# Layer 2 of a four-layer cross-attention kernel: another mask instruction, the layer norm on other engines, the weights transposed one tile later, and its last tiles beside layer 3

## The chip, the cores and the metric

The kernel runs on one core of one Trainium2 chip. Its engines work side by side, each through its own instructions in order: TensorE (PE in the profile, with its weight loads as PEld), VectorE (DVE), ScalarE (ACT), GpSimd (POOL) and SyncE (SP), which issues the DMAs here. They wait for each other by semaphores. The metric is the time of one execution in device microseconds; less is better.

## The reference

Four layers of cross-attention follow each other on x (4 batches, 1024 rows of 256); the context has 77 rows in each batch. The change is in layer 2 and at its seam with layer 3:

```python
# layer 2: 16 heads of 16; mask and factors come as inputs (4, 16, 1024, 77)
scores = einsum('bhqd,bhkd->bhqk', q, k) / sqrt(16) * attention_weights
scores = where(attention_mask, -inf, scores)
out = softmax(scores) @ v                       # heads side by side again
x = x + out @ Wo.T + bo
x = (x - mean(x)) * rsqrt(var(x) + 1e-5) * gamma + beta
# layer 3: 16 heads of 64, no mask
normed = x * rsqrt(mean(x * x) + 1e-6) * norm_w
x = x + softmax((normed @ wq) @ (ctx @ wk).T) @ (ctx @ wv) @ wo
```

Layers 0 and 1 (self- and cross-attention with a feed-forward part; Taylor linear attention with a window) take the first three quarters of the time and are not touched.

## The kernel before, in words

The order of all work is written out by hand; the instructions of each engine stand in the order of the program text. Layers 2 and 3 work in tiles of 128 rows, 32 in all, eight to a batch. The output projection is folded into the values beforehand (`U`: one row of 256 for each head and context row), so a tile has one score matrix `s` of 128 x 1232 (16 heads of 77), its transpose `pT` in ten pieces, and one product `po` of `pT` with `U`.

A function `slots` calls `slot2` for i = 0 to 34 and then `slot3` for i = 0 to 33. One call is called a slot; it issues parts of several tiles. `slot2(i)` issues, in this order:

- the loads of factors and mask (`side`) for tile i+1, and a new `s` for tile i (one of three buffers; POOL clears its last 48 columns, L1288);
- for tile i-1 sixteen exponentials on ScalarE, one for each head, with the maximum `nm` as bias (L1363);
- for tile i the scores on TensorE (`ps`, L45), the product with the factors on VectorE (L1375, two halves, from PSUM), and the mask in one VectorE instruction: mask times -1e30 plus s (L1380; the mask is of 8-bit numbers);
- side jobs up to a given share of the batch (`gap2`);
- for tile i-3 the product `po` (ten matrix multiplies, shown as twenty records);
- for tile i the maximum of each head (L1392, L1396);
- for tile i-2 the ten transposes `psT` (L1283) and their three copies out of PSUM on ScalarE (L1284);
- for tile i-3 the addition of `po` to x on VectorE (L1402) and of the bias row `bo` on GpSimd (L1403);
- side jobs again;
- for tile i-1 the sums and their reciprocals on VectorE (L1408, L1409), and the scaling of `s` by them on GpSimd (L1410).

Side jobs are generators, each advanced in small steps between two given shares of a batch of eight slots. In layer 2 they are: `prep2` (transposes x of the next batch, `ptx`, copied by VectorE, L340, and projects it, `pp`, copied by ScalarE, L1332); `norm2(b-1)`, the layer norm of the batch before, which begins at share 0.45 with `bn_stats` and `bn_aggr` of eight tiles on VectorE (L298, L299), goes on with a short chain on GpSimd that makes rs = (var + 1e-5) to the power -0.5 (L289, L290), and then treats one tile a step by two VectorE instructions (L1421, L1425); and during the last batch the first batch of layer 3, `stats3(0)` and `features3(0)` (L313, `ptx`, L342). `norm2` of the last batch is a job of layer 3's first batch.

`slot3(i)` is alike, with a lag of two: scores `ps` with `G`, maximum and subtraction on VectorE (L1480, L1481), one exponential for all heads (L1489), sums, reciprocals and scaling (L1492 to L1494), transposes, `po`, the addition (L1504) and the store of the finished tile.

PSUM has two tiles for `ps` (`pair_tile`), three for `psT`, `ptx` and `pp` together, and one for `po`; so a `po` begins only when L1402 has read the one before.

Of the kernel before, what the change touches and what calls it, by code (L numbers as in the profile page):

```python
# [10 lines left out]
F32 = mybir.dt.float32  # L11
# [20 lines left out]
def tile_xattn_seq(ctx: ExitStack, tc: tile.TileContext, d: dict, out: bass.AP):  # L32
# [65 lines left out]
    def load_cols_of(*keys):  # L98
        for key, n in keys:
            cols[key] = cpool.tile([P, n], F32, name="c_" + key)  # L100
            load_cols(cols[key], d[key])

    load_cols_of(("L0_xattn_g1", 2), ("L0_xattn_be1", 2))
    nhalf = cpool.tile([P, NT], F32, name="nhalf")
    nc.gpsimd.memset(nhalf, -0.5)

# [1177 lines left out]
        nc.scalar.copy(pT[:, 4 * group : 4 * group + n, :], ps[:, 0:n, :])  # L1284

    def new_scores():
        s = late.tile([P, P * NC], F32, name="s", tag="s", bufs=3)
        nc.gpsimd.memset(s[:, HK:], 0.0)  # L1288
        return s

# [56 lines left out]

    def slot2(i, tiles, at, gap2):

        p1, p2, p3 = tiles.get(i - 1), tiles.get(i - 2), tiles.get(i - 3)  # L1350
        a = None
        if i < NB * NT:
            b, t = divmod(i, NT)
            a = tiles[i] = dict(b=b, t=t)
            qT, kb = shared["b2", b], shared["k2"]
            fs, mk = shared.pop(("side", i))
            if i + 1 < NB * NT:
                load_sides(i + 1)
            s = a["s"] = new_scores()
        if p1:  # L1360
            for h in range(H):
                hs = p1["s"][:, S * h : S * h + S]
                nc.scalar.activation(hs, hs, AF.Exp, bias=p1["nm"][:, h : h + 1], scale=SC)  # L1363
        if a:
            for o in range(2):
                ps = pair_tile()
                for e in range(2):
                    r = half_rows(e)
                    mm(
                        ps[:, e, 0 : 4 * S].rearrange("p (h s) -> p h s", s=S),  # L1370
                        qT[r, o, P * t : P * t + P],
                        kb[r, o, :, b, :],
                    )
                so = slice(o * HH * S, (o + 1) * HH * S)
                nc.vector.tensor_tensor(  # L1375
                    s[:, so].rearrange("p (i n) -> p i n", i=2), ps[:, :, 0 : 4 * S],
                    fs[:, so].rearrange("p (i n) -> p i n", i=2), ALU.mult,
                )
            sv = s[:, 0:HK]
            nc.vector.scalar_tensor_tensor(sv, mk, NEG, sv, op0=ALU.mult, op1=ALU.add)  # L1380
        gap2(at + 0.4)
        if p3:
            U = shared["u2", p3["b"]]
            xt = xs[p3["b"]][:, p3["t"], :]
            po = pvp.tile([P, D], F32, name="po2", tag="pv")
            for c in range(NC):
                r = slice(0, rows_in(c))
                mm(po, p3["pT"][r, c, :], U[r, c, :], start=(c == 0), stop=(c == NC - 1))
            del tiles[i - 3]
        if a:  # L1390
            nm = a["nm"] = small.tile([P, H], F32, name="nm", tag="m16")
            nc.vector.tensor_reduce(  # L1392
                nm, sv.rearrange("p (h k) -> p h k", k=S), axis=AX.X, op=ALU.max
            )

            nc.vector.tensor_scalar(nm, nm, 0.1 * NEG, -SC, ALU.max, ALU.mult)  # L1396
        if p2:
            pT = p2["pT"] = late.tile([P, NC, P], F32, name="pT", tag="pT")
            for g in range(3):
                turned(p2["s"], g, pT)  # L1400
        if p3:
            nc.vector.tensor_tensor(xt, po, xt, ALU.add)  # L1402
            nc.gpsimd.tensor_tensor(xt, xt, rows["bo"], ALU.add)  # L1403
        gap2(at + 1.0)
        if p1:
            s3 = p1["s"][:, 0:HK].rearrange("p (h k) -> p h k", k=S)
            den = small.tile([P, H], F32, name="den", tag="den")
            nc.vector.tensor_reduce(den, s3, axis=AX.X, op=ALU.add)  # L1408
            nc.vector.reciprocal(den, den)  # L1409
            nc.gpsimd.tensor_tensor(  # L1410
                s3, s3, den.unsqueeze(2).to_broadcast([P, H, S]), ALU.mult
            )

    def norm2(b):

        x = xs[b]
        res = []
        yield from stats_job(res, lambda t: x[:, t, :], 1e-5, False)
        mv, rs = res
        for t in range(NT):  # L1420
            nc.vector.scalar_tensor_tensor(  # L1421
                x[:, t, :], x[:, t, :], mv[:, t, 0:1], rows["gamma"],
                op0=ALU.subtract, op1=ALU.mult,
            )
            nc.vector.scalar_tensor_tensor(  # L1425
                x[:, t, :], x[:, t, :], rs[:, t : t + 1], rows["beta"],
                op0=ALU.mult, op1=ALU.add,
            )
            yield


# [23 lines left out]
    def slot3(i, tiles, at, gap2):  # L1455
        a, p2 = None, tiles.get(i - 2)
        if i < NB * NT:
            b, t = divmod(i, NT)
            a = tiles[i] = dict(b=b, t=t)
            G, _ = shared["b3", b]  # L1460
            xT = shared["xT3", b]
            s = a["s"] = new_scores()
            m = small.tile([P, H], F32, name="m3", tag="m16")
        if p2:
            pT = late.tile([P, NC, P], F32, name="pT", tag="pT")
        for o in range(2):
            if p2:
                turned(p2["s"], o, pT)
            if a:
                ps = pair_tile()  # L1470
                for e in range(2):
                    k0 = (2 * o + e) * 4 * S
                    for c in range(2):
                        mm(
                            ps[:, e, 0 : 4 * S], xT[:, c, P * t : P * t + P],
                            G[:, c, k0 : k0 + 4 * S], start=(c == 0), stop=(c == 1),
                        )
                pv = ps[:, :, 0 : 4 * S].rearrange("p i (h s) -> p i h s", s=S)
                mo = m[:, HH * o : HH * o + HH].rearrange("p (i h) -> p i h", i=2)
                nc.vector.tensor_reduce(mo, pv, axis=AX.X, op=ALU.max)  # L1480
                nc.vector.tensor_tensor(  # L1481
                    s[:, HH * S * o : HH * S * (o + 1)].rearrange("p (i h s) -> p i h s", i=2, s=S),
                    pv, mo.unsqueeze(3).to_broadcast([P, 2, 4, S]), ALU.subtract,
                )
        if p2:
            turned(p2["s"], 2, pT)
        gap2(at + 0.5)
        if a:
            nc.scalar.activation(s[:, 0:HK], s[:, 0:HK], AF.Exp)  # L1489
            s3 = s[:, 0:HK].rearrange("p (h k) -> p h k", k=S)  # L1490
            den = small.tile([P, H], F32, name="den", tag="den")
            nc.vector.tensor_reduce(den, s3, axis=AX.X, op=ALU.add)  # L1492
            nc.vector.reciprocal(den, den)  # L1493
            nc.gpsimd.tensor_tensor(  # L1494
                s3, s3, den.unsqueeze(2).to_broadcast([P, H, S]), ALU.mult
            )
        if p2:
            U = shared["b3", p2["b"]][1]
            xt = xs[p2["b"]][:, p2["t"], :]
            po = pvp.tile([P, D], F32, name="po3", tag="pv")  # L1500
            for c in range(NC):
                r = slice(0, rows_in(c))
                mm(po, pT[r, c, :], U[r, c, :], start=(c == 0), stop=(c == NC - 1))
            nc.vector.tensor_tensor(xt, po, xt, ALU.add)  # L1504
            nc.sync.dma_start(out=out[p2["b"], P * p2["t"] : P * p2["t"] + P, :], in_=xt)
            del tiles[i - 2]
        gap2(at + 1.0)
# [156 lines left out]
    run(loads2(0))  # L1664
    run(prep2(0))

    def slots(slot, lag, jobs_of):
        tiles = {}
        for i0 in range(0, NB * NT + lag, NT):
            b = i0 // NT  # L1670
            jobs = jobs_of(b)
            n = min(NT, NB * NT + lag - i0)

            def gap2(share):
                for j in jobs:
                    j.run(share / n)

            for k in range(n):
                slot(i0 + k, tiles, k, gap2)
            for j in jobs:  # L1680
                j.end()

    def jobs2(b):
        j = []
# [11 lines left out]
    def jobs3(b):  # L1696
        j = []
        if b == 0:
            j.append(Job(norm2(NB - 1), 16, 0.0, 1.0))
        if b + 1 < NB:  # L1700
            j.append(Job(stats3(b + 1), 8, 0.0, 0.4))
            j.append(Job(features3(b + 1), 8, 0.45, 0.95))
            j.append(Job(loads3(b + 1), 1, 0.4, 0.41))
        return j

    slots(slot2, 3, jobs2)
    slots(slot3, 2, jobs3)


# [28 lines left out]
```

## Time and profile before

| | |
|---|---|
| median of three runs | 2509.88 us (2508.1 to 2509.99) |
| the profiled execution | time 2512.11 us, span 2510.4 us |
| PE, DVE, ACT, POOL busy over the span | 92%, 58%, 41%, 24% |
| first mask of layer 2 | 1880.1 us |
| last `po` of layer 2 ends | 2190.5 us |
| DMA over the span | 39 GB/s on the mean |

All profile times are of the one profiled execution; microseconds count from the start of its span. In the windows each row gives a stretch, its length, the busy time of each engine with the number of instructions, the granted TensorE clock (1 is full), the share of DMA, and GB/s. In the groups a row is one line of the kernel on one engine: output and inputs by name, shapes and count, then busy time, the mean ns of one, and the idle time of that engine before them with what ended it. The waits name who waited for whom. The timeline gives start and duration of single instructions or of a few of one kind, merged.

### The profile page before, as it was taken

Reading aid. Unit: us, or ns where it says so; the run is one execution under the profiler, and the core shown is the slowest. Engines: PE = TensorE matmul, PEld = TensorE weight load, DVE = VectorE, ACT = ScalarE, POOL = GpSimd, SP = SyncE. Lnnn points to the kernel's source line nnn. Section 1 sums busy time; section 2 is a strip of 40 time slices with the busy share of each in tenths; the row PEclk is TensorE's granted clock in tenths of the full one; section 3 lists DMA queues with packets and bytes.
Section 4 is the critical chain, followed back from the end, with each engine's and each line's share of the span. In section 5 each row is a group of like instructions: output and inputs, shape, how many; then the busy total and the mean of one; then the engine's idle time right before and its main releaser. Section 6 shows DMA issues by size and latency. Waiting matters only on the chain.

```text
span 2510.4 us, 39752 instructions
## 1 busy us (share of the span) xinstructions
PE 2301.8 (92%) x16162; PEld 1387.1 (55%) x16162; DVE 1446.8 (58%) x2411; ACT 1019.0 (41%) x1684; POOL 595.5 (24%) x850
## 2 busy tenths in 40 slices
PE   5789989898989989899999999999988997899999
PEld 3433433444444444444556766656656665678887
DVE  4446456654565444664346435454438999797664
ACT  1234344333443344334443434444436665322222
POOL 2001013111130111311152223333323333332222
PEclk9799999999999999999999999999998999899999
DMA  6412021100000000100000010101013333012200
GB/s 169 117 26 91 10 75 36 41 6 14 2 7 12 6 14 6 22 14 5 14 15 9 14 23 16 19 15 19 15 67 120 109 109 117 26 52 54 55 14 17
DMA packets 87136, 98.49 MB, mean 39 GB/s; under 512 B 31222, under 2 KB 77866, under 8 KB 86826
## 3 DMA queue, kind: packets, MB, share of 16 engines
q1 hardware_dynamic: 86954, 95.95, 14.7%
q8 instruction: 128, 2.10, 0.3%
q14 instruction: 54, 0.44, 0.1%
HBM read 57.70 MB, written 20.59 MB: 31 GB/s over the span
## 4 chain that ended last, share of the span: by engine, by line
PE 77%; DVE 13%; ACT 5%; issue 2%; DMA 1%; POOL 1%; SPq 0%; ACTq 0%; DVEq 0%; POOLq 0%
PE ps L45 32%; PE po L45 15%; PE pp L45 6%; PE pv L45 5%; DVE mpart L599 5%; PE ph L45 4%; PE ppv L45 2%; PE psT L1283 2%; PE pvw L45 2%; ACT pe L664 2%; PE ptx L336 1%; DVE s L1380 1%; PE pvl L45 1%; PE pk L45 1%; PE pt L540 1%
## 5 line engine op out<-in xcount | busy, mean ns | idle before, releaser
L45 PE MATMUL ps<-qk 32*128 32x192 f32 (+8 forms) x5760 | 618.5, 470 | 101.5 <-DVE mpart L599 54.3
L664 ACT ACTIVATE pe<-ps 128x1024 f32<-128x1024 f32 (+2 forms) x384 | 363.0, 951 | 614.8 <-PE ps L45 609.6
L599 DVE TENSOR_REDUCE mpart<-ps 128x2 f32<-128x1024 f32 (+3 forms) x448 | 409.2, 933 | 352.3 <-PE ps L45 351.7
L45 PEld LDWEIGHTS ps<-qk 32*128 32x128 f32 (+1 forms) x5760 | 288.9, 186 | 373.3 <-DVE mpart L599 133.4
L45 PE MATMUL po<-U,pT 128*128 128x256 f32 (+1 forms) x1280 | 296.9, 388 | 15.5 <-DVE x L1402 13.9
L45 PEld LDWEIGHTS po<-U,pT 128*128 128x128 f32 (+1 forms) x1280 | 244.1, 194 | 60.7 <-issue 21.2
L667 POOL TENSOR_SCALAR_AFFINE_SELECT pe<-pe 128x256 f32<-128x256 f32 (+1 forms) x192 | 95.1, 496 | 635.5 <-ACT pe L664 622.1
L1054 DVE TENSOR_REDUCE mrow<-ps 128x4 f32<-128x768 f32 x128 | 122.5, 957 | 141.4 <-PE ps L45 141.0
L1284 ACT COPY pT<-psT 128x512 f32<-128x512 f32 (+1 forms) x192 | 92.4, 518 | 268.8 <-PE psT L1283 268.8
L1129 ACT ACTIVATE pew<-ps 128x768 f32<-128x768 f32 x128 | 103.3, 811 | 172.3 <-PE ps L45 171.5
L1134 POOL TENSOR_SCALAR_AFFINE_SELECT pew<-pew 128x512 f32<-128x512 f32 x128 | 81.7, 638 | 342.7 <-ACT pew L1129 342.7
L45 PE MATMUL pv<-pe,va 128*32 128x512 f32 (+3 forms) x1536 | 162.0, 510 | 0.1
L45 PE MATMUL ps<-G,xT 128*128 128x308 f32 x512 | 143.7, 425 | 0.0
L1363 ACT ACTIVATE s<-s,nm 128x77 f32<-128x77 f32 x512 | 131.3, 348 | 28.3 <-DVE nm L1396 28.2
L45 PE MATMUL ph<-yT,w 128*128 128x256 f32 x512 | 139.3, 408 | 0.8 <-DVE qk L525 0.8
L1494 POOL TENSOR_TENSOR s<-s,den 128x1232 f32<-128x1232 f32 x32 | 72.0, 2250 | 222.7 <-DVE den L1493 194.7
L45 PEld LDWEIGHTS ph<-yT,w 128*128 128x128 f32 x512 | 94.3, 199 | 52.2 <-issue 38.3
L45 PE MATMUL po<-w,hT 128*128 128x256 f32 x512 | 118.3, 384 | 0.0
L1283 PE MATMUL psT<-ident,s 128*128 128x128 f32 x640 | 93.8, 279 | 23.9 <-POOL s L1410 20.4
L45 PEld LDWEIGHTS ps<-G,xT 128*128 128x128 f32 x512 | 93.1, 192 | 27.5 <-issue 0.9
L45 PEld LDWEIGHTS po<-w,hT 128*128 128x128 f32 x512 | 96.3, 192 | 21.8 <-issue 9.5
L525 DVE TENSOR_TENSOR qk<-pm,qk 128x512 f32<-128x512 f32 x64 | 44.1, 689 | 106.7 <-PE pm L523 106.7
(187 smaller groups left out, 3140.3 us busy)
## 6 DMA issues: line engine op xcount, KB each, us to landing
side<-in_fside_t SPq DMA_DIRECT2D x32, 616.0 KB
qk<-st SPq DMA_DIRECT2D x256, 64.0 KB
U<-kept_u SPq DMA_DIRECT2D x8, 1152.0 KB
side<-in_mask_t SPq DMA_DIRECT2D x32, 154.0 KB
G<-kept_g SPq DMA_DIRECT2D x4, 1232.0 KB
x<-in_x SPq DMA_DIRECT2D x8, 512.0 KB
out<-x SPq DMA_DIRECT2D x32, 128.0 KB
kept_u<-st SPq DMA_DIRECT2D x21, 154.0 KB
```

Source lines behind the costliest of these rows:

```text
L45: nc.tensor.matmul(o, lhsT, rhs, start=start, stop=stop, **kw)
L525: nc.vector.tensor_tensor(qs, pm.rearrange("p i n -> p (i n)"), qs, ALU.add)
L599: nc.vector.tensor_reduce(mpart[bl][:, i, 2 * p : 2 * p + 2, ci], ps[:, :, o : o + w], axis=AX.X, op=ALU.max,)
L664: nc.scalar.activation(pp[:n, :, o:512], ps[:n, :, o:512], AF.Exp, scale=SC)
L667: nc.gpsimd.affine_select(out=own, in_=own, compare_op=ALU.is_ge, fill=0.0, base=0, pattern=[[0, 2], [0, k], [1, P]], channel_multiplier=-1,)
L1054: nc.vector.tensor_reduce(mo, ps.rearrange("p j (i n) -> p j i n", i=2)[:, :, :, 0 : P + WIN], axis=AX.X, op=ALU.max, negate=True,)
L1129: nc.scalar.activation(pp[:, :, :, 0 : P + WIN], ps.rearrange("p j (i n) -> p j i n", i=2)[:, :, :, 0 : P + WIN], AF.Exp, scale=SC,)
L1134: nc.gpsimd.affine_select(out=pf[:, :, 0:P], in_=pf[:, :, 0:P], compare_op=ALU.is_ge, fill=0.0, base=0, pattern=[[0, 4], [1, P]], channel_ ...
L1283: nc.tensor.transpose(ps[:, k, :], s[:, P * c : P * c + P], ident)
L1284: nc.scalar.copy(pT[:, 4 * group : 4 * group + n, :], ps[:, 0:n, :])
L1363: nc.scalar.activation(hs, hs, AF.Exp, bias=p1["nm"][:, h : h + 1], scale=SC)
L1494: nc.gpsimd.tensor_tensor(s3, s3, den.unsqueeze(2).to_broadcast([P, H, S]), ALU.mult)
```

## The change

The mask becomes a predicated copy of a constant (`low`, one column of -1e30, read as a broadcast) into s where the mask is set. The layer norm of a tile becomes one ScalarE activation, x times rs plus `away` = -mean times rs, and two GpSimd instructions, times gamma and plus beta. The transposes of a tile move one slot later (tile i-3 in slot i) and `po` with its additions too (tile i-4); `s` has four buffers instead of three, and `pT` three instead of two, in layers 2 and 3. The four slots of layer 2 that have no new tile are no longer issued by themselves: each goes ahead of one of the first four slots of layer 3, without side jobs. The norm of the last batch starts at share 0.1 of layer 3's first batch instead of 0.0.

```diff
+    low = cpool.tile([P, 1], F32, name="low")
+    nc.gpsimd.memset(low, NEG)
...
-        s = late.tile([P, P * NC], F32, name="s", tag="s", bufs=3)
+        s = late.tile([P, P * NC], F32, name="s", tag="s", bufs=4)
...
-        p1, p2, p3 = tiles.get(i - 1), tiles.get(i - 2), tiles.get(i - 3)
+        p1, p3, p4 = tiles.get(i - 1), tiles.get(i - 3), tiles.get(i - 4)
...
-            nc.vector.scalar_tensor_tensor(sv, mk, NEG, sv, op0=ALU.mult, op1=ALU.add)
+            nc.vector.copy_predicated(sv, mk, low.to_broadcast([P, HK]))
...
-        if p3:
-            U = shared["u2", p3["b"]]
-            xt = xs[p3["b"]][:, p3["t"], :]
+        if p4:
+            U = shared["u2", p4["b"]]
+            xt = xs[p4["b"]][:, p4["t"], :]
...
-                mm(po, p3["pT"][r, c, :], U[r, c, :], start=(c == 0), stop=(c == NC - 1))
+                mm(po, p4["pT"][r, c, :], U[r, c, :], start=(c == 0), stop=(c == NC - 1))
...
-        if p2:
-            pT = p2["pT"] = late.tile([P, NC, P], F32, name="pT", tag="pT")
+        if p3:
+            pT = p3["pT"] = late.tile([P, NC, P], F32, name="pT", tag="pT", bufs=3)
             for g in range(3):
-                turned(p2["s"], g, pT)
-        if p3:
+                turned(p3["s"], g, pT)
+        if p4:
             nc.vector.tensor_tensor(xt, po, xt, ALU.add)
...
         mv, rs = res
+        away = small.tile([P, NT], F32, name="away", tag="away")
+        nc.gpsimd.tensor_tensor(away, mv[:, :, 0], rs, ALU.mult)
+        nc.gpsimd.tensor_scalar(away, away, -1.0, None, ALU.mult)
         for t in range(NT):
-            nc.vector.scalar_tensor_tensor(
-                x[:, t, :], x[:, t, :], mv[:, t, 0:1], rows["gamma"],
-                op0=ALU.subtract, op1=ALU.mult,
+            xt = x[:, t, :]
+            nc.scalar.activation(
+                xt, xt, AF.Identity, bias=away[:, t : t + 1], scale=rs[:, t : t + 1]
             )
-            nc.vector.scalar_tensor_tensor(
-                x[:, t, :], x[:, t, :], rs[:, t : t + 1], rows["beta"],
-                op0=ALU.mult, op1=ALU.add,
-            )
+            nc.gpsimd.tensor_tensor(xt, xt, rows["gamma"], ALU.mult)
+            nc.gpsimd.tensor_tensor(xt, xt, rows["beta"], ALU.add)
             yield
...
-    def slots(slot, lag, jobs_of):
+    def slots(slot, lag, jobs_of, ending=None):
...
+            for k in range(NT):
+                if ending:
+                    next(ending, None)
                 slot(i0 + k, tiles, k, gap2)
...
+        def rest():
+            for i in range(NB * NT, NB * NT + lag):
+                slot(i, tiles, 0, lambda share: None)
+                yield
+
+        return rest()
...
-            j.append(Job(norm2(NB - 1), 16, 0.0, 1.0))
+            j.append(Job(norm2(NB - 1), 16, 0.1, 1.0))
...
-    slots(slot2, 3, jobs2)
-    slots(slot3, 2, jobs3)
+    run(slots(slot3, 2, jobs3, slots(slot2, 4, jobs2)))
```

More of the change, by code (lines that the diff above doesn't have):

```diff
@@ L1387, in slot2 @@
                 r = slice(0, rows_in(c))
-                mm(po, p3["pT"][r, c, :], U[r, c, :], start=(c == 0), stop=(c == NC - 1))
-            del tiles[i - 3]
+                mm(po, p4["pT"][r, c, :], U[r, c, :], start=(c == 0), stop=(c == NC - 1))
+            del tiles[i - 4]
         if a:
@@ L1464, in slot3 @@
         if p2:
-            pT = late.tile([P, NC, P], F32, name="pT", tag="pT")
+            pT = late.tile([P, NC, P], F32, name="pT", tag="pT", bufs=3)
         for o in range(2):
@@ L1665, in tile_xattn_seq @@
     run(prep2(0))
-    def slots(slot, lag, jobs_of):
+    def slots(slot, lag, jobs_of, ending=None):
         tiles = {}
[L1669 to L1672, printed above, removed]
+        for i0 in range(0, NB * NT, NT):
+            jobs = jobs_of(i0 // NT)
             def gap2(share):
                 for j in jobs:
-                    j.run(share / n)
-            for k in range(n):
+                    j.run(share / NT)
+            for k in range(NT):
+                if ending:
+                    next(ending, None)
                 slot(i0 + k, tiles, k, gap2)
```

## The prediction

> **What bounds the kernel now.** I read the windows first, cut at the first mask of each batch of layer 2 (eight slots), then DVE's groups, the waits, and one slot of the timeline.
>
> ```profile
> core 0: us, PE busy (x) PEld busy (x) DVE busy (x) ACT busy (x) POOL busy (x), PEclk, DMA share, GB/s
> 1880.00:1942.00 62.00, 52.73 (x261) 38.53 (x258) 54.34 (x64) 41.24 (x144) 18.56 (x18) 0.89 0.38 123
> 1942.00:2018.00 76.00, 69.31 (x349) 52.02 (x347) 71.48 (x102) 47.39 (x163) 27.17 (x27) 0.98 0.31 101
> 2018.00:2094.00 76.00, 68.42 (x336) 50.70 (x336) 70.77 (x100) 45.68 (x156) 26.73 (x27) 0.96 0.31 100
> 2094.00:2176.00 82.00, 60.94 (x303) 46.78 (x304) 76.83 (x123) 43.81 (x152) 28.59 (x31) 0.93 0.30 89
> ...
> 2214.00:2510.00 296.00, 293.21 (x1437) 240.10 (x1435) 198.89 (x299) 82.81 (x122) 78.48 (x73) 1.00 0.15 41
> ```
>
> The rows are the four batches of layer 2, then layer 3. Layer 3 belongs to PE (293 of 296 us): what is taken off DVE there is worth nothing. In layer 2 DVE is 93% to 94% busy from the second batch on, and ACT and POOL are at most 62% and 36% busy there.
>
> ```profile
> line engine op names shapes xcount | busy us, mean ns | idle before us <-releasers
> L1380 DVE SCALAR_TENSOR_TENSOR s<-side,s 128x1232 f32<-128x1232 uint8 x32 | 68.9, 2153 | 1.1
> L1425 DVE SCALAR_TENSOR_TENSOR x<-x,rs,r_beta 128x256 f32<-128x256 f32 x24 | 13.7, 571 | 6.4 <-POOL rs L290 5.7
> L1402 DVE TENSOR_TENSOR x<-po,x 128x256 f32<-128x256 f32 x29 | 12.1, 419 | 4.7 <-PE po L45 4.7
> L1421 DVE SCALAR_TENSOR_TENSOR x<-x,mv,r_gamma 128x256 f32<-128x256 f32 x24 | 11.8, 493 | 0.0
> ```
> ```profile
> engine line waited for: us in total, times, longest us
> PE psT L1283 <- POOL s L1410: 20.4, 11, 6.5
> PE po L45 <- DVE x L1402: 13.9, 9, 2.6
> ```
> ```profile
> 2006.18 1.44 DVE L1375 TENSOR_TENSOR s<-ps,side 128x616 f32<-128x616 f32 x2
> 2006.41 2.25 POOL L1410 TENSOR_TENSOR s<-s,den 128x1232 f32<-128x1232 f32 x1 [2.98 <-ACT s L1363]
> 2007.66 2.30 DVE L1380 SCALAR_TENSOR_TENSOR s<-side,s 128x1232 f32<-128x1232 uint8 x1
> ...
> 2009.88 0.47 DVE L1421 SCALAR_TENSOR_TENSOR x<-x,mv,r_gamma 128x256 f32<-128x256 f32 x1
> 2010.38 0.49 DVE L1425 SCALAR_TENSOR_TENSOR x<-x,rs,r_beta 128x256 f32<-128x256 f32 x1
> 2010.79 1.43 DVE L1392 TENSOR_REDUCE nm<-s 128x16 f32<-128x1232 f32 x1
> ```
>
> The first group rows count DVE's work in layer 2 before 2176 us. The waits (1880 to 2203 us) show PE waiting for POOL's scaling, but in DVE's slots PE is the one with slack, so that wait is not on the path. In the timeline DVE runs without a hole. The mask (L1380, 1.44 us alone, 2.3 as a rule) starts while POOL scales s, and ends 1.3 us after POOL: it stands still until POOL is done.
>
> **Part 1, the norm leaves DVE.** 24 of the 32 pairs L1421/L1425 stand in layer 2 (8 in layer 3, worth nothing). From start to start on DVE a pair takes 0.91 us (0.51 + 0.40), two a batch 1.27 (L1425 held up behind POOL's bo add L1403, 0.83 instead of 0.48), and the first 2.92, 1.88 of them waiting for POOL's rs. A batch: 5 x 0.91 + 2 x 1.27 + 2.92 = 10.0 us; three batches 30.0. All lie on the engine that sets the pace: -30.0.
>
> Is PE next? A slot's PE work is read from the chain where PE runs unbroken (6.85 us a slot near 1925): psT 1.09, ps 1.24, po 4.52. Preparing the next batch adds 4 x 0.66 (ptx) + 4 x 1.95 (pp) = 10.4 us. The second and third batch need 8 x 6.85 + 10.4 = 65.2 us of PE, and DVE keeps 75.7 - 10.0 = 65.7 and 66.1: just level. The fourth has 82.5 - 10.0 = 72.5 on DVE, 57.4 on PE. So the whole 30 comes through, but little beyond it would in the middle batches.
>
> What it adds: 24 ScalarE activations of 128x256. None is in the trace; the near rows are L1363 (77 wide, 348 ns) and L1489 (1232 wide, 1230 ns), so 0.49 us each by a straight line, about 0.4 back to back (16 exps of 0.348 take 4.1 us, so each hides 0.09 of the next): 3.2 us a batch on an engine with 29 us idle. They stand in ACT's queue ahead of the exps, and the first of a batch waits for POOL's rs (pow 1.67 us) and the two small ops for "away" (about 0.2 each, by L285 and L287). At 1990 us, where DVE waits for rs now, ACT would be held to about 1994 instead of starting the exps of the next slot at 1990.83; they take 4.1, and the den of that tile comes on DVE about 3.2 us after they are due to end. I book 1 us of stall a batch: +3 (0 to 6).
>
> POOL gets 48 TENSOR_TENSOR of 128x256 at 763 ns (L1403's mean): 12.2 us a batch on top of 27 of 76. They stand ahead of the s scaling L1410 in POOL's queue, and hold it by up to two tiles, 3 us. Its reader, the transposes, now comes a slot later, which covers that; without that slot PE would be late by those 3 us.
>
> Here the skill speaks against the change. The Trainium skill, "Perfetto Trace Analysis", Optimizing Scalar/DVE Operations, says that GpSimd and DVE share an SBUF read port, so moving work between these two may not help. If each of the 48 held DVE, 48 x 0.76 = 36 us would eat the 30. The row says who is held: L1425 and L1380 behind POOL, but L1375 (one input in PSUM) keeps 0.77 us beside L1410, and the reductions keep 1.42. After the change only the mask and the few xn copies are exposed, once a slot, in 9 slots, to a piece of at most 0.76: 7 us by the worst case; at half the time in the way and half a piece each about 2. I take +2.
>
> **Part 2, the mask as a predicated copy.** No such instruction is in the trace. The nearest row is L1380 with the same shape and mask: 1441 ns alone, 2295 behind POOL. The Trainium skill, "SBUF — State Buffer", Who interferes with whom, says that a DVE instruction with two SBUF inputs contends with a GpSimd instruction that reads SBUF. Mask and value both lie in SBUF, so by the rule the copy stalls as L1380 does. By the row alone it could also run at 1.44 throughout. Low end: 32 x (2.15 - 1.44) = 23 us off DVE, of which PE's level lets through about 6 in the fourth batch and 4 in the others: -10. High end: two cycles an element where L1380 has one: 1441 + 1232/0.96 GHz (the unstalled rate, 1232 in some 1283 ns) = 2.73, + 0.71 stall: 32 x 1.29 = +41. I take L1380's price: 0.
>
> **Part 3, a tile later, and a fourth s and third pT.** PE, ACT and DVE do the same work, in other slots. The loads of side, U and G keep their slots on SP's queue, and POOL's memset of a new s still waits for transposes of the slot before, as the fourth buffer goes with the later turn: 0 for both. In the first batch PE is behind: DVE waits there for ps 1.84 and 1.88 and for po 2.02. One po and psT less (5.6 us) by its end relieves that by about half: -3 (0 to -6).
>
> **Part 4, the seam.** Before: from where mask 32 would stand (2176.6) to the end 333.8 us, in which PE runs on but for 3.2 us before layer 3's first psT and some 3 us of a po at a granted clock near 0.6 (7.54 instead of 4.56). After: PE has one tile more left, +5.6, and layer 3's scores fill the 3.2 and, with PE kept busier, I expect the slow po away: 5.6 - 3.2 - 3 = -0.6; taken as 0 (-3 to +4). The overlap is worth little because PE was hardly idle in the drain.
>
> Sum: -30 + 3 + 2 + 0 - 3 + 0 = -28. The profiled execution has a span of 2510.4 and a time of 2512.1 (1.7 around it); 2482.4 + 1.7 = 2484.1. It ran 2.2 above the median of the three runs, 2509.9, so for the median 2482.
>
> **Rivals.** (a) *The copy escapes POOL's hold.* For: L1375 runs beside L1410 unharmed. Against: two SBUF operands, as L1380. -28 - 10: 2472. (b) *The predicated copy is dear.* It turns the sign from the point where it costs 28/32 = 0.9 us more than L1380, so from about 3.0 us in the mean; at 3.44 us (2.73 + 0.71) it gives -28 + 41 = +13: 2523, slower. For: a third operand, the old s, may be read. Against: L1380 too reads two and writes one at one element a cycle. (c) *ACT's and POOL's queues become the bound in the norm slots*: scaling waits for beta, beta for ACT, ACT behind copies that wait for PE. If half of the 30 comes back: 2497; all of it: 2512. For: PE waits for L1410 already, 20.4 us. Against: the slot of slack, and POOL at 36%.
>
> **How the numbers follow.** 5 us (0.2%) is about what a measurement of this kernel tells from no change. As worked out 0.57 (2474 to 2492), (a) 0.15, (b) 0.14, (c) 0.14, of it 0.08 faster, 0.05 within 0.2%, 0.01 counted with it. Faster: 0.57 + 0.15 + 0.08 = 0.80; same 0.05; slower 0.15, nearly all (b). The range leaves out (b) and the far half of (c): 2464 to 2502.
>
> **What would show it.** Right: the mask's mean near 2.1 us; no gamma or beta on DVE; the last slots of each batch down from 10.3-11.2 to about 7.3 us; the three later batches near 66, 66 and 73 us; PE's wait for L1410 gone. Wrong: a mask mean over 3 us, or under 1.6; DVE waiting for ACT's exps before the den; slots still near 10 us where the norm stands.

## The result and the profile after

The changed kernel takes 2470.31 us (median of 4 runs, 2467.84 to 2472.59) beside 2508.99 us of the kernel before: a ratio of 0.9862, 95% interval 0.9835 to 0.9889. That is 38.7 us less; the forecast was 28 less, 2482, in a range (2464 to 2502) that holds the result. The course as worked out had 2474 to 2492, so the result lies outside it: it is rival (a) that came true, within 2 us of its 2472. The mask does not wait for POOL.

The windows of the changed kernel, cut again at the first mask of each batch of layer 2, and layer 3 as the last row:

```profile
core 0: us, PE busy (x) PEld busy (x) DVE busy (x) ACT busy (x) POOL busy (x), PEclk, DMA share, GB/s
1877.00:1934.00 57.00, 46.74 (x228) 31.99 (x227) 52.20 (x63) 38.71 (x137) 17.84 (x17) 0.91 0.41 134
1934.00:2001.00 67.00, 65.73 (x343) 49.95 (x342) 60.17 (x86) 48.23 (x162) 32.90 (x39) 1.00 0.35 114
2001.00:2067.00 66.00, 64.33 (x336) 48.75 (x335) 60.03 (x84) 48.64 (x164) 37.71 (x44) 1.00 0.35 116
2067.00:2137.00 70.00, 59.90 (x320) 47.93 (x320) 63.93 (x107) 49.27 (x171) 43.37 (x54) 0.98 0.35 105
2176.00:2470.00 294.00, 291.69 (x1431) 238.93 (x1429) 187.18 (x279) 86.56 (x129) 85.97 (x85) 1.00 0.13 36
```

The second and third batch have changed hands: DVE fell from 71 us to 60, PE is busy 64 to 66 of 66 to 67 us, and its clock is full. The fourth is still DVE's, 64 of 70 us. Layer 3 is as before.

VectorE's groups in layer 2 (1880 to 2140 us, so 31 of the 32 masks), and two waits (1880 to 2170 us):

```profile
line engine op names shapes xcount | busy us, mean ns | idle before us <-releasers
L1383 DVE COPY_PREDICATED_SCALAR s<-side,low 128x1232 f32 x31 | 49.7, 1602 | 1.1
L1405 DVE TENSOR_TENSOR x<-po,x 128x256 f32<-128x256 f32 x29 | 12.1, 417 | 9.3 <-PE po L45 8.9
L1399 DVE TENSOR_SCALAR nm<-nm 128x16 f32<-128x16 f32 x32 | 8.9, 277 | 1.1
```
```profile
engine line waited for: us in total, times, longest us
ACT x L1428 <- POOL away L1425: 11.2, 3, 6.9
PE po L45 <- DVE x L1405: 4.7, 5, 1.2
```

Line 1383 is the old 1380. The copy's mean is 1602 ns where the multiply-add had 2153. PE's wait of psT for POOL's scaling (20.4 us before) is gone from this view; what is left of psT's waits is for ACT, 2.7 us. ACT waits for `away` as foreseen, 11.2 us at three times. And `nm`, a step on 16 elements, has become dearer: 277 ns in the mean, 175 before. The timeline shows both sides of it:

```profile
1984.63 1.44 DVE L1378 TENSOR_TENSOR s<-ps,side 128x616 f32<-128x616 f32 x2
...
1986.11 1.60 DVE L1383 COPY_PREDICATED_SCALAR s<-side,low 128x1232 f32 x1
...
1986.67 0.73 POOL L1431 TENSOR_TENSOR x<-x,r_gamma 128x256 f32<-128x256 f32 x1 [0.72 <-ACT x L1428]
1987.48 0.72 POOL L1432 TENSOR_TENSOR x<-x,r_beta 128x256 f32<-128x256 f32 x1
...
1988.16 2.25 POOL L1413 TENSOR_TENSOR s<-s,den 128x1232 f32<-128x1232 f32 x1
...
1989.22 1.30 DVE L1399 TENSOR_SCALAR nm<-nm 128x16 f32<-128x16 f32 x1
```

POOL's gamma runs inside the mask's time and neither is longer for it. But `nm`, due 0.17 us, ends at 1990.52, 0.11 us after POOL's scaling.

**Lengths of the batches.** Executions of one kernel lie up to 21 us apart (2495.4 to 2516.0 for the kernel before on one chip). A part of that is made ahead of layer 2: the first mask starts between 1868.7 and 1883.9 us in the twelve profiles, although nothing but a memset of the constant is changed before it. So the steps are compared by the lengths of layer 2's batches in each profiled execution: from the start of the 1st mask to that of the 9th, 17th and 25th, and from there to where a 33rd would start (a mask starts 1.64 us after the start of the reciprocal ahead of it where nothing stands between them). The tail is the rest of the span. Each row is one execution. `changed` and `seam_apart`, whose code is the same up to the end of batch 4, agree within 0.1 us in batches 2 to 4 and differ by 1.5 us in the first.

| kernel | batch 1 | 2 | 3 | 4 | sum | tail |
|---|---|---|---|---|---|---|
| before | 62.2 | 75.7 | 76.1 | 82.5 | 296.5 | 333.9 |
| changed | 56.7 | 66.7 | 66.3 | 69.3 | 259.0 | 334.3 |
| mask_alone | 61.5 | 74.9 | 72.8 | 76.3 | 285.5 | 333.0 |
| all_but_mask | 59.4 | 66.8 | 66.6 | 76.0 | 268.8 | 336.0 |
| mask_full_tile | 61.5 | 66.8 | 66.6 | 76.6 | 271.5 | 334.4 |
| order_alone | 58.0 | 75.7 | 75.1 | 82.5 | 291.3 | 333.8 |
| norm_alone | 61.8 | 70.1 | 73.3 | 75.8 | 281.0 | 337.9 |
| norm_nm_scalar | 61.0 | 70.9 | 74.1 | 72.0 | 278.0 | 336.8 |
| turn_early | 62.6 | 70.8 | 70.8 | 69.3 | 273.5 | 332.3 |
| seam_apart | 58.2 | 66.7 | 66.3 | 69.3 | 260.5 | 338.9 |
| stats_early | 56.7 | 66.7 | 66.6 | 64.7 | 254.7 | 334.3 |
| stats_early_nm_scalar | 56.3 | 66.8 | 66.9 | 63.6 | 253.6 | 334.2 |

Of the 39.5 us between the two profiled spans, 37.5 lie in the four batches, 2.4 ahead of the first mask, and the tail is 0.4 longer. Lengths and tails together lie within the intervals of the whole times given below, for all runs but `norm_alone` and `norm_nm_scalar`, where the whole time gives less.

### The profile page after: what moved, and what is told of

The parts are those of the page before. It is cut to its first block, busy times and chain, and to the rows that moved or that the text cites. A ratio compares the mean times of both kernels' runs of the same rounds, so it can differ in the third digit from the quotient of the medians.

```text
span 2470.9 us, 39772 instructions
## 1 busy us (share of the span) xinstructions
PE 2284.0 (92%) x16162; PEld 1376.6 (56%) x16162; DVE 1398.5 (57%) x2347; ACT 1033.3 (42%) x1716; POOL 640.5 (26%) x923
## 4 chain that ended last, share of the span: by engine, by line
PE 78%; DVE 11%; ACT 6%; issue 2%; POOL 1%; DMA 1%; SPq 1%; ACTq 0%; DVEq 0%; POOLq 0%
PE ps L45 33%; PE po L45 15%; PE pp L45 6%; PE pv L45 5%; DVE mpart L601 5%; PE ph L45 4%; PE ppv L45 2%; PE psT L1285 2%; PE pvw L45 2%; ACT pe L666 2%; PE ptx L338 1%; PE pvl L45 1%; PE pk L45 1%; PE pt L542 1%; PE pm L525 1%
## 5 line engine op out<-in xcount | busy, mean ns | idle before, releaser
L45 PE MATMUL po<-U,pT 128*128 128x256 f32 (+1 forms) x1280 | 290.5, 382 | 7.4 <-DVE x L1405 4.7
L818 DVE TENSOR_SCALAR hT<-ph,c_L_xattn_b 128x256 f32<-128x256 f32 x128 | 61.3, 480 | 72.4 <-PE ph L45 65.2
```

The lines of the kernel that those rows point to most:

```text
L45: nc.tensor.matmul(o, lhsT, rhs, start=start, stop=stop, **kw)
L818: nc.vector.tensor_scalar(h[:, f, :], ph, cols["L0_xattn_b1"][:, 4 * half + f : 4 * half + f + 1], None, ALU.add,)
```

## Experiments

Each ratio below is to runs of the kernel before on the same chip, with its 95% interval. Their median was 2509.01 us for the first four experiments, 2505.17 for norm_alone, turn_early, seam_apart and stats_early, and 2501.14 for the two with `nm` on ScalarE; so times of different groups are compared by their ratios.

**mask_alone**

```diff
-            nc.vector.scalar_tensor_tensor(sv, mk, NEG, sv, op0=ALU.mult, op1=ALU.add)
+            nc.vector.copy_predicated(sv, mk, low.to_broadcast([P, HK]))
```

> The kernel before with the predicated copy alone; norm, turn and seam as before. Theory M (the mask is the part that was sized wrongly: the copy takes 1.60 us in every slot and does not wait for POOL): DVE loses 32 x (2.15 - 1.60) = 17.6 us in layer 2, of which the first batch, where PE is late, keeps a part: 13 to 17 us faster, about 2494. Rival O (the surplus over the forecast comes from the order, the fill of the first batch and a warmer clock, and the mask is hidden): not more than 4 us faster.

2493.82 us, ratio 0.9943 (0.9926 to 0.9960). The instructions of the mask line in it:

```profile
L1382 DVE COPY_PREDICATED_SCALAR s<-side,low x32: 1585/1598/1611, 1875.7 to 2151.6; 128x1232 f32 x32
```

Minimum, median and maximum lie within 26 ns: in 32 slots it never waited, though POOL's scaling runs beside it in 26 of them (28 before). Theory M; rival O falls.

**all_but_mask**: the changed kernel with those two lines the other way round.

> The changed kernel with the mask put back as multiply and add. Theory M: the masks stall behind POOL again, and the time is that of the forecast, which took no gain for the mask: about 2482, 11 us above the changed kernel. Rival O: about 2473, within 4 us of it.

2485.73 us, ratio 0.9908 (0.9875 to 0.9940): nearer to theory M's 2482 than to rival O's 2473.

```profile
L1381 DVE SCALAR_TENSOR_TENSOR s<-side,s x32: 1441/2155/3515, 1880.2 to 2140.6; 128x1232 f32<-128x1232 uint8 x32
```

This is the kernel that the forecast described, one whose mask is priced as before. The batches say where the mask's part lies: against the changed kernel 2.7 us in the first, 0.1 and 0.3 in the two that are PE's, 6.7 in the fourth, 9.8 in all. The busy time of the mask and of `nm` together is 2.8, 5.0, 4.3 and 7.5 us longer here in these batches, so VectorE gets as much in the middle ones and keeps next to nothing of it. The tail is 1.7 longer as well.

**mask_full_tile**

```diff
-            nc.vector.copy_predicated(sv, mk, low.to_broadcast([P, HK]))
+            nc.vector.copy_predicated(sv, mk, low)      # low: 128 x 1232 of -1e30
```

> The changed kernel, but the value that the copy sets is read from a full 128 x 1232 tile of -1e30 instead of one column read as a broadcast. If the copy is free of POOL because its value is a single column per partition (one stream from SBUF left), the full tile brings the stall back: mean near 2.2 us a mask, about 2481 us. If the predicated copy never meets POOL whatever its value, it stays at 1.60 us and the time within 3 us of the changed kernel.

2480.71 us, ratio 0.9894 (0.9853 to 0.9936).

```profile
L1381 DVE COPY_PREDICATED s<-side,low x32: 1531/2236/3612, 1876.6 to 2139.4; 128x1232 f32<-128x1232 uint8 x32
```

The profile names another form of the operation, without SCALAR. It is the quicker one when alone (1531 against 1592 ns) and waits like the multiply-add. So it isn't the predicated copy as such that is free of POOL, but its form with one value for each partition. Why is not shown: the profile names no inputs' shapes for that form, and "one stream from SBUF left" stays a reading. The first and fourth batch are long again, 61.5 and 76.6 us.

**order_alone**: the kernel before with the later turn, the buffers and the seam of the changed kernel.

```diff
-        p1, p2, p3 = tiles.get(i - 1), tiles.get(i - 2), tiles.get(i - 3)
+        p1, p3, p4 = tiles.get(i - 1), tiles.get(i - 3), tiles.get(i - 4)
...
+    run(slots(slot3, 2, jobs3, slots(slot2, 4, jobs2)))
```

> The kernel before with the later turn, the fourth s, the third pT and the seam beside layer 3; mask and norm as before. Theory M and the forecast: -3 in the first batch, 0 at the seam, so 2503 to 2509. Rival O: 10 us or more faster, below 2499.

2504.54 us, ratio 0.9984 (0.9968 to 0.9999). 4.2 us come out of the first batch, 1.0 of the third, nothing of the others or of the tail. The time lies where the forecast had it; rival O falls. Later turn, buffers and seam were not taken apart any further here.

**norm_alone**: the kernel before with the norm on ScalarE and GpSimd.

```diff
-            nc.vector.scalar_tensor_tensor(
-                x[:, t, :], x[:, t, :], mv[:, t, 0:1], rows["gamma"],
-                op0=ALU.subtract, op1=ALU.mult,
-            )
...
+            nc.scalar.activation(
+                xt, xt, AF.Identity, bias=away[:, t : t + 1], scale=rs[:, t : t + 1]
+            )
+            nc.gpsimd.tensor_tensor(xt, xt, rows["gamma"], ALU.mult)
+            nc.gpsimd.tensor_tensor(xt, xt, rows["beta"], ALU.add)
```

> The kernel before with the norm on ScalarE and GpSimd alone; mask as before, transposes and po in their old slots, three s, two pT, seam apart. If the norm's 30 us come through without the later turn (theory N): 30 less 3 for ACT's wait and 2 for POOL's hold, about 2484. If the later turn is what covers the scaling that now stands behind gamma and beta (theory T, the forecast's 3 us for each of 9 slots): up to 27 us come back less DVE's share, 2491 to 2500, and PE waits for the scaling longer than the 20.4 us of before.

2501.29 us, ratio 0.9974 (0.9959 to 0.9990): less even than theory T gave. In the profiled execution layer 2 is 15.5 us shorter and the tail 4.0 longer, 11.5 in all; the whole times give 3.9 us, at most 10.3 by the interval. What takes the difference is open, so these lengths say where the gain lies better than how large it is. Two things in its trace could have eaten the rest. The waits (1870 to 2200 us):

```profile
engine line waited for: us in total, times, longest us
PE psT L1283 <- POOL s L1410: 28.8, 12, 7.5
DVE s L1375 <- PE ps L45: 13.0, 11, 6.8
```

and the step `nm` in the timeline, behind POOL's scaling, with the groups' row for all 32:

```profile
1999.71 2.25 POOL L1410 TENSOR_TENSOR s<-s,den 128x1232 f32<-128x1232 f32 x1
1999.87 2.19 DVE L1396 TENSOR_SCALAR nm<-nm 128x16 f32<-128x16 f32 x1
```
```profile
L1396 DVE TENSOR_SCALAR nm<-nm x32: 174/175/2199, 1886.8 to 2160.3; 128x16 f32<-128x16 f32 x32
```

Gamma and beta stand ahead of the scaling in POOL's queue, so in these slots it no longer falls on the mask but on `nm`, and PE gets it later too.

**norm_nm_scalar** was made to tell these two apart.

```diff
+            nc.scalar.activation(p1["nm"], p1["nm"], AF.Identity, scale=-SC)
...
-            nc.vector.tensor_scalar(nm, nm, 0.1 * NEG, -SC, ALU.max, ALU.mult)
```

> norm_alone, with the small step on the maxima (nm, 128x16, on VectorE a tensor_scalar) as one ScalarE activation ahead of the exponentials; its clamp at -1e29, which only a row masked entirely would need, is left out. In norm_alone that step stood still behind the scaling in 8 slots, 13 us in all. Theory L (this hold on VectorE is what ate the norm's gain): 13 us of stall and 32 x 0.09 us of the step itself leave VectorE, about 2486. Theory P (the transposes' wait for the scaling, 28.8 us on TensorE, is what ate it, and VectorE would only wait elsewhere): less than 5 us, 2496 to 2502.

2498.44 us, ratio 0.9985 (0.9963 to 1.0006), by itself not to be told from the kernel before nor from norm_alone (the lengths give 15.6 less than before, outside the interval, and again it is open why). Layer 2 is 3.0 us shorter than norm_alone's: 3.8 less in the fourth batch and 0.8 in the first, 0.8 more in each of the two between, though 13 us of standing still are gone. VectorE now waits for PE's scores instead (L1375 in norm_alone, L1376 here; 6.8 us of either lie ahead of the first mask). The waits, and the windows of the two middle batches:

```profile
PE psT L1283 <- POOL s L1410: 28.6, 13, 7.3
DVE s L1376 <- PE ps L45: 21.8, 12, 6.8
```
```profile
1939.00:2010.00 71.00, 65.12 (x333) 48.46 (x332) 60.82 (x77) 50.41 (x170) 37.51 (x42) 0.98 0.33 108
2010.00:2084.00 74.00, 69.36 (x340) 51.91 (x339) 60.29 (x77) 51.57 (x173) 41.00 (x46) 0.95 0.31 103
```

In these windows PE's wait for the scaling is 5.8 and 4.5 us; with its busy time that makes 70.9 of 71 and 73.9 of 74 us, and VectorE is busy for 61 and 60. So theory P holds for the two middle batches: without the later turn PE's work and its wait for the scaling set their end, and the hold of `nm` only fills the same time. A part of PE's busy time in the third is its clock, 0.95 where the changed kernel has 1.00; whether the waits lower the clock is not shown. In the fourth, DVE's own, the hold counted.

**turn_early**: the changed kernel with the old lag.

```diff
-        p1, p3, p4 = tiles.get(i - 1), tiles.get(i - 3), tiles.get(i - 4)
+        p1, p2, p3 = tiles.get(i - 1), tiles.get(i - 2), tiles.get(i - 3)
...
-    run(slots(slot3, 2, jobs3, slots(slot2, 4, jobs2)))
+    run(slots(slot3, 2, jobs3, slots(slot2, 3, jobs2)))
```

> The changed kernel with transposes and po in their old slots (lag of three), all else kept: four s, three pT, predicated copy, norm, seam beside layer 3. Theory T: 5.6 us less PE work is left at the seam, but PE waits for the scaling in the norm slots: 4 us or more slower than the changed kernel, 2474 to 2485. Theory N: the wait is covered anyway and the shorter end wins: 2464 to 2468.

2484.45 us, ratio 0.9913 (0.9884 to 0.9942). Theory T: PE waits for the scaling again,

```profile
PE psT L1285 <- POOL s L1413: 24.1, 10, 7.9
```

and the first three batches are 5.9, 4.1 and 4.5 us longer. In the second and third, where the norm stands, this wait is 4.2 and 4.3 us. The first batch has no norm; its wait is a single one of 7.9 us, which the kernel before has too (6.5), and order_alone gained 4.2 there. The fourth is the same to a tenth, since DVE has it. The tail is 2.0 us shorter: the tile less that PE has left at the seam.

**seam_apart**

```diff
-    run(slots(slot3, 2, jobs3, slots(slot2, 4, jobs2)))
+    run(slots(slot2, 4, jobs2))
+    run(slots(slot3, 2, jobs3))
```

> The changed kernel with the four last slots of layer 2 issued by themselves ahead of layer 3. The forecast (PE has work in the drain, the overlap is worth 3 us for layer 3's first transposes and at most 3 of a slow clock): 2472 to 2477. If the overlap is what carries the surplus: 2480 or more.

2478.44 us, ratio 0.9892 (0.9864 to 0.9921), 1.4 above what the forecast gave, and more by the ratio, as this chip's kernel before is 3.8 us faster; so the whole time does not decide between the two, and the lengths have to. Its tail is 4.6 us longer than the changed kernel's, and 1.5 of its surplus fell into the first batch, which the edit doesn't touch. PE's timeline at its seam:

```profile
2153.06 4.59 PE L45 MATMUL po<-U,pT 128*128 128x256 f32 x20
2157.48 8.46 PE L45 MATMUL ps<-G,xT 128*128 128x308 f32 x32
2169.06 1.11 PE L1285 MATMUL psT<-ident,s 128*128 128x128 f32 x4 [3.12 <-POOL s L1498]
```

PE runs through the drain and then stands 3.12 us for layer 3's first scaled tile. Right behind that hole its clock is at half for 3 us (the window below), which costs about another 1.5; the two make the 4.6. In the changed kernel layer 3's first psT waits for 0.17 us, and the clock from 2139 to 2176 us is 1.00:

```profile
2169.00:2172.00 3.00, 2.94 (x8) 2.26 (x9) 2.67 (x7) 1.21 (x2) 0.08 (x2) 0.50 0.00 0
```
```profile
2158.63 0.63 PE L1285 MATMUL psT<-ident,s 128*128 128x128 f32 x4 [0.17 <-ACT pT L1286]
```

**stats_early**, a version meant to beat both: the fourth batch of the changed kernel is DVE's and the third is PE's, so work of DVE is moved from the one into the other.

```diff
+        if b == NB - 2:
+            j.append(Job(stats3(0), 8, 0.0, 0.4))
         if b == NB - 1:
-            j.append(Job(stats3(0), 8, 0.0, 0.3))
```

> The changed kernel with the statistics of layer 3's first batch (eight pairs of bn_stats and bn_aggr, 0.53 us each on VectorE) in the third batch of layer 2 instead of the fourth. If the fourth batch is still DVE's (64 of 71 us busy) and the third is PE's (64 of 66), 4.2 us leave the path: 2465 to 2468. If the fourth batch is held by something else, or the third by DVE too: within 2 us of the changed kernel.

2467.11 us, ratio 0.9851 (0.9819 to 0.9883). The interval overlaps the changed kernel's, so the times do not show it faster. In the profiled execution the step is seen (third and fourth batch):

```profile
2002.00:2068.00 66.00, 64.12 (x335) 48.43 (x334) 62.69 (x100) 48.57 (x163) 39.59 (x49) 1.00 0.36 116
2068.00:2133.00 65.00, 59.36 (x319) 47.73 (x318) 60.89 (x92) 48.54 (x168) 40.71 (x48) 0.97 0.39 113
```

The fourth batch is 4.6 us shorter, the third 0.3 longer, with 2.7 us more of DVE under PE's 64.

**stats_early_nm_scalar**: the same with `nm` on ScalarE.

> stats_early with the same step on ScalarE, the clamp left out in the same way. Its stalls there are 2.95 us in 5 slots, the step itself 32 x 0.09 us; two of the batches are TensorE's, so 1 to 3 us of the 6 come through: about 2465. If ScalarE, which has one more small instruction a slot ahead of the exponentials, becomes the bound: 2468 or more.

2468.38 us, ratio 0.9846 (0.9812 to 0.9881). Layer 2 is 1.1 us shorter than in stats_early: the fourth batch by 1.1, the first by 0.4, the middle ones 0.4 longer together; the whole time can't tell the two apart.

## Why the prediction was right, and where it was off

**The mask was the mis-sized term.** The forecast took 0, L1380's price, because mask and value both lie in SBUF. Measured: 1.60 us in each slot, no stall. Alone (mask_alone) that is 0.55 us less in the mean, 32 times, 17.7 us off DVE, of which 11.0 came out of the batches. In the changed kernel, against all_but_mask, it is 13.2 us off the mask and 6.4 off the holds of `nm`, of which 9.8 came out, and 1.7 more in the tail. Rival (a) had 10, 6 in the fourth batch and 4 in the others: it measured 6.7 and 3.1. So the reading of which batches let a gain through was right, and the doubt about the instruction was resolved the wrong way. The rule of the Trainium skill ("SBUF — State Buffer", Who interferes with whom), that two SBUF inputs meet a GpSimd instruction which reads SBUF, fits mask_full_tile, whose value is a full tile: median 2236 ns. With the value as one column it gave the wrong answer, as it was read: 1.60 us throughout.

Rival (b) fell: it had priced a second cycle for each element, 2.73 us at least, and the copy takes 1.60, 0.16 more than L1380 alone. (The rate in that sum can be estimated from the kernel before: L1396 takes 174 ns for 16 elements and L1380 1441 for 1232, so 1.04 ns an element.) Rival (c) did not show in the changed kernel, whose middle batches end where PE's own work ends; without the later turn half of the norm's 30 us was missing in the batches, as it feared.

**The rest of the sum nearly held, in part because two errors went against each other.** all_but_mask is that sum without the mask: 25.4 us less span than before, forecast 28. The norm gave 4.7 less than booked (20.3 with its tail) and order and seam 2.3 more (5.3).

- *The norm.* -30 + 3 + 2 = -25 was booked; all_but_mask against order_alone is 22.5 us shorter in layer 2 and 2.2 longer in the tail, where nothing was booked; why is open. PE became the next bound where it was expected: 66.7 and 66.3 us for the middle batches, forecast "near 66", with 65.7 and 64.3 us of PE where 65.2 were reckoned. The last three slots of these batches came down to 7.2 to 7.8 us, forecast 7.3.
- *The hold by POOL.* Size and victim were wrong. The mask and the copies xn were named as all that is exposed; the small step `nm` is, too. It stood 9.7 us in all_but_mask (32 steps, above 0.175 each) and 3.3 in the changed kernel. In all_but_mask the mask itself was held 6.1 us less than in order_alone, so the net is 3.6 against the 2 booked. The rule that speaks against such a move ("Perfetto Trace Analysis", Optimizing Scalar/DVE Operations) shows in these stalls, but the 48 instructions cost far less than the 36 us of the worst case.
- *ACT's wait.* `away` held ACT 11.2 us at three times, but no sum (`den`) of layer 2 waited for ACT's exponentials in the changed kernel; two waited 0.9 us together for beta. Of the 3 booked little was paid.
- *The later turn.* "Without that slot PE would be late by those 3 us" was right in kind: in turn_early PE waits 4.2 and 4.3 us in the two middle batches, two waits of at most 2.6 us in each, and the batches are 4.1 and 4.5 longer. norm_alone shows only 15.5 of the 22.5. The first batch gained 4.2 by the order alone, forecast 3.
- *The seam.* 0 was booked as +5.6 - 3.2 - 3. The tail changed by 0.4: seam_apart has 5.0 more than before, about one tile, and the overlap takes 4.6 of it back.
- *The fourth batch* was forecast at 73. It was 76.0 with the mask as before, the holds being larger than booked, and came to 69.3 by the mask's 6.7.

Of the 39.5 us between the two spans, 2.4 lie ahead of the first changed slot, and I call them chance, not gain.

## What to carry to other kernels

Take work off the engine that sets the pace stage by stage, and stop counting where the next engine is level: here the copy took 5.0 and 4.3 us off VectorE in two batches and gave 0.1 and 0.3, and 7.5 in another and gave 6.7. When work moves to a shared in-order queue, look at what stands behind it and give its reader a slot more; in the profiled executions this norm, moved alone, gave 15.5 us of layer 2, and on top of the later turn 22.5, though turn, buffers and seam without it gave 5. The whole times make the first of these smaller still. A constant that an instruction takes as one column instead of a full tile may be another form of it, with other neighbours: look at the operation's name in the trace.

## What was not expected of the hardware

- The predicated copy with one value a partition takes 1.60 us for 128x1232 and runs beside a GpSimd instruction unharmed; with a full tile it takes 1.53 us at its shortest, 2.24 in the median and up to 3.61.
- A VectorE step on 16 elements, 0.17 us, lasted up to 2.20 us behind a GpSimd instruction of 2.25, while the reductions of 1232 elements (L1392, L1395) kept to 1.40 to 1.44 in every slot.
- A ScalarE activation of 128x256 with scale and bias by column took 0.60 us, two in a row 1.07 to 1.11; the straight line through its neighbours had given 0.49, and about 0.4 back to back.
